# Layer 0, second pass: score blocks above the diagonal loaded as 32-squares to their transposed place and turned by VectorE

## The chip, the cores and the metric

The kernel runs on one core of a Trainium2 chip. The metric is the device time of one execution in microseconds. A core has five engines that run their own instruction streams and wait for each other by semaphores: TensorE (PE, with PEld for its weight loads), VectorE (DVE), ScalarE (ACT), GpSimd (POOL) and SyncE (SP). Transfers run on 16 DMA engines; SP and POOL issue them. SBUF and PSUM are the on-chip memories; TensorE writes PSUM.

## The reference

Two graph layers, one after the other, on a feature array `x` of 4096 x 512 with a 4096 x 4096 adjacency `adj`. The change is in the first. Cut to what matters:

```python
h = jnp.maximum(_layernorm(x), 0.0)
node_att = softmax(h @ node_w, axis=0)
he = h @ edge_w
e = he @ he.T                              # 4096 x 4096 scores, symmetric
e = jnp.where(adj > 0, e, NEG_BIG)
edge_att = softmax(e, axis=1)
output = adj * (node_att * edge_att) @ (h @ weight)
x = x + output + bias
# then layer 1: a graph attention layer with 8 heads of 64, same N and adj
```

Everything is 32-bit floating point. The scores before the mask are symmetric: `e` and its transpose are the same array.

## The kernel before, in words

With P = 128 rows to a tile there are NT = 32 row tiles; BL = 512 columns make a block, NB = 8 blocks, TB = 4 tiles in a block.

**First pass** (to about 707 us). Score tiles are computed for blocks on and above the diagonal only (L285), and each 128 x 512 tile `es` is written to an HBM array `e_d` (L289, issued by POOL). Row maxima are collected for the softmax. The lower half of `e_d` is never written.

**Second pass** (about 707 to 1650 us, `load`, `turn`, `exps`, `weigh`, `gather`). It loops over blocks b of 512 output rows and, inside, over the 32 row tiles m of neighbours. A step (b, m) needs the scores with neighbours on the partitions: the 128 x 512 tile whose rows are the neighbours of tile m and whose columns are the outputs of block b. Where m lies left of the block (m // 4 < b) this tile is in `e_d` as it stands and is loaded as `et` (L350). On the diagonal (m // 4 == b) a trapezoid of four parts is loaded into `eb` (L346), and what is missing is turned by TensorE. Right of the block (m // 4 > b, "above the diagonal") only the transposed block exists: one DMA loads 512 x 512 scores for four steps into `eb` (L354), and in each of those steps TensorE turns four 128 x 128 tiles into a PSUM tile `pt` (L370).

- `load(b, m)`, 8 steps ahead: the DMAs above, all on SP's queue, and that of the adjacency tile `a` (L358).
- `turn(b, m)`, 3 ahead: the transposes.
- `exps(b, m)`, 2 ahead: VectorE makes a mask `mk` from `a` (L378), subtracts the row maxima `mb` from the scores (L381, from PSUM or SBUF to `d`) and adds the mask (L382); ScalarE takes the exponential (L384).
- `weigh(b, m)`, 1 ahead: VectorE multiplies by the adjacency into `at` (L390); GpSimd adds up the row sum `racc` (L400).
- `gather(b, m)`, 0 ahead: TensorE multiplies `at` into the four PSUM accumulators `po` (L420), eight matmul instructions a step[...].

The order is written out by hand: for every step the stages are recorded in this sequence, so on each engine and each queue the instructions stand in this order and are executed in it. Pools set how far a stage can run ahead: `eb` has 4 buffers, `a` 11, `pt` 3 PSUM banks, `at` 3. A DMA on SP's queue waits, before it is issued, for the buffer it fills and for the DMA issued eight before it. At the end of the pass the next layer's preparation is mixed into row block 7, which has no step above the diagonal.

**Layer 1** (from about 1650 us) does not touch what is changed.

Of the kernel before, what the change touches and what calls it, by code (L numbers as in the profile page):

```python
# [8 lines left out]
FP = mybir.dt.float32  # L9
AF = mybir.ActivationFunctionType  # L10
ALU = mybir.AluOpType
# [4 lines left out]
P = 128  # L16
# [6 lines left out]
def row_bcast(ap, n, offset=0):  # L23

    return bass.AP(tensor=ap.tensor, offset=ap.offset + offset, ap=[[0, P], [1, n]])
# [3 lines left out]
def kernel(  # L29
# [15 lines left out]
    nc = tc.nc  # L45
    N, F = x.shape
# [5 lines left out]
    BL = 512  # L52
    NB = N // BL
    TB = BL // P

    const = ctx.enter_context(tc.tile_pool(name="const", bufs=1))
    dram = ctx.enter_context(tc.tile_pool(name="dram", bufs=1, space=DRAM))
# [13 lines left out]

    e_d = dram.tile([N, N], FP, name="e_d")
    mx_d = [dram.tile([TB, P], FP, name=f"mx_d{b}") for b in range(NB)]
    xb_d = dram.tile([N, F], FP, name="xb_d")
    big = ctx.enter_context(tc.tile_pool(name="l0", bufs=1))
# [19 lines left out]
    with tc.tile_pool(name="w0", bufs=1) as wp, tc.tile_pool(name="a0", bufs=2) as ap_, tc.tile_pool(  # L97
        name="a0s", bufs=8
# [38 lines left out]
        def turn(t):  # L137
            b, j = divmod(t, TB)
            if j == 0:
                hts[b] = ap_.tile([P, KC, BL], FP, name="h_t")  # L140
            h = hs.pop(t)
            pt = pp.tile([P, KC, P], FP, name="pt")
            for k in range(KC):
                nc.tensor.transpose(pt[:, k, :], h[:, k * P:(k + 1) * P], ident)  # L144
            nc.vector.tensor_copy(hts[b][:, :, j * P:(j + 1) * P], pt)
            hw = sp.tile([P, F], FP, name="hw", bufs=1)
            nc.vector.tensor_tensor_reduce(hw, h, nw_b, 1.0, 0.0, ALU.mult, ALU.add, lg[:, t:t + 1])
            xb = sp.tile([P, F], FP, name="xb", bufs=1)
            nc.gpsimd.tensor_tensor(xb, xts.pop(t), bias_b, ALU.add)
            nc.gpsimd.dma_start(xb_d[t * P:(t + 1) * P, :], xb)  # L150
# [92 lines left out]
    with tc.tile_pool(name="mx", bufs=1) as mxp, tc.tile_pool(name="b_a", bufs=6) as adjp, tc.tile_pool(  # L243
        name="b_e", bufs=4
    ) as esp, tc.tile_pool(name="b_m", bufs=2) as mkp, tc.tile_pool(name="b_s", bufs=2) as sp, tc.tile_pool(
        name="b_p", bufs=6, space=PSUM
# [11 lines left out]
        def load(i, j, t):  # L258
            w, lo, sk = parts(i, j, t)
            rows = slice(t * P, (t + 1) * P)  # L260
            ar = adjp.tile([P, BL], FP, name="ar")
            nc.sync.dma_start(ar[:, :w], adj[rows, lo:lo + w])
            ac = None
            if w > sk:
                ac = adjp.tile([P, BL], FP, name="ac")
                nc.sync.dma_start(ac[:, sk:w], adj_t[rows, lo + sk:lo + w])
            loaded[i, j, t] = ar, ac
# [35 lines left out]
        for n in range(-6, len(items)):  # L303
# [3 lines left out]
            if n >= 0:  # L307
                i, j, t = items[n]
# [9 lines left out]
    with tc.tile_pool(name="c_a", bufs=11) as adjp, tc.tile_pool(name="c_b", bufs=4) as ebp, tc.tile_pool(  # L318
        name="c_e", bufs=9
    ) as etp, tc.tile_pool(name="c_w", bufs=3) as wkp, tc.tile_pool(name="c_t", bufs=3) as atp, tc.tile_pool(  # L320
        name="c_m", bufs=2
    ) as mxp, tc.tile_pool(name="c_o", bufs=4) as iop, tc.tile_pool(name="c_s", bufs=2) as sp, tc.tile_pool(
        name="c_p", bufs=1, space=PSUM
    ) as p_o, tc.tile_pool(name="c_q", bufs=3, space=PSUM) as p_t, tc.tile_pool(
        name="c_r", bufs=1, space=PSUM
    ) as p_r, tc.manual_schedule():
        steps = [(b, m) for b in range(NB) for m in range(NT)]
        blk = {}
        src, aj, ex, at = {}, {}, {}, {}

        def rows_of(m):
            return slice(m * P, (m + 1) * P)

        def load(b, m):
            cols = slice(b * BL, (b + 1) * BL)
            if m == 0:
                mb = mxp.tile([P, BL], FP, name="mb") if b else mb_0
                if b:
                    nc.gpsimd.dma_start(mb, row_bcast(mx_d[b], BL))
                blk[b] = [mb, None, None, None]  # L340
            if m // TB == b:
                if m % TB == 0:
                    eb = ebp.tile([P, TB, BL], FP, name="eb")
                    for i in range(TB):
                        q = (m + i) * P
                        nc.sync.dma_start(eb[:, i, i * P:], e_d[q:q + P, q:(b + 1) * BL])  # L346
                        src[b, m + i] = eb
            elif m // TB < b:
                et = etp.tile([P, BL], FP, name="et")
                nc.sync.dma_start(et, e_d[rows_of(m), cols])  # L350
                src[b, m] = et
            elif m % TB == 0:
                eb = ebp.tile([P, TB, BL], FP, name="eb")
                nc.sync.dma_start(eb, e_d[cols, m * P:m * P + BL].rearrange("(j p) f -> p j f", p=P))  # L354
                for i in range(TB):
                    src[b, m + i] = eb
            a = adjp.tile([P, BL], FP, name="a")
            nc.sync.dma_start(a, adj_t[rows_of(m), cols])  # L358
            aj[b, m] = a

        def turn(b, m):

            i = m % TB
            n = TB if m // TB > b else i if m // TB == b else 0
            eb = src[b, m]
            parts = []
            if n > 0:
                pt = p_t.tile([P, BL], FP, name="pt")
                for j in range(n):
                    nc.tensor.transpose(pt[:, j * P:(j + 1) * P], eb[:, j, i * P:(i + 1) * P], ident)  # L370
                parts.append((slice(0, n * P), pt))
            if n < TB:
                parts.append((slice(n * P, BL), eb[:, i, :] if m // TB == b else eb))
            src[b, m] = parts

        def exps(b, m):
            mk = wkp.tile([P, BL], FP, name="mk")
            nc.vector.tensor_scalar(mk, aj[b, m], 0.0, NEG_BIG, ALU.is_le, ALU.mult)  # L378
            d = wkp.tile([P, BL], FP, name="d")
            for cs, part in src.pop((b, m)):  # L380
                nc.vector.tensor_tensor(d[:, cs], part[:, cs], blk[b][0][:, cs], ALU.subtract)  # L381
            nc.vector.tensor_tensor(d, d, mk, ALU.add)  # L382
            e = wkp.tile([P, BL], FP, name="ex")
            nc.scalar.activation(e, d, AF.Exp)  # L384
            ex[b, m] = e
# [44 lines left out]
        def finish():  # L430

            t, acc, oc, rs, xt = left.pop(0)
            b, j = divmod(t, TB)
            if j == 0:
                sc = sp.tile([P, TB], FP, name="sc")
                nc.vector.reciprocal(sc, rs)
                nc.vector.tensor_tensor(sc, sc, na[:, b * TB:(b + 1) * TB], ALU.mult)
                scale[b] = sc
            nc.vector.scalar_tensor_tensor(oc, acc, scale[b][:, j:j + 1], xt, op0=ALU.mult, op1=ALU.add)
            nc.gpsimd.dma_start(x1[rows_of(t), :], oc)  # L440
# [71 lines left out]
        end = len(steps)  # L512

        def tail(s):

            if s == -6:
                w_fetch()
            if -6 <= s and s + 6 < NT:
                fetch(s + 6)
            if s == -2:  # L520
                stats(0)
                stats(1)
                norm(0)
                stats(2)
                norm(1)
            if s >= 0:
                if 0 < s:
                    values(s - 1)
                if s + 2 < NT:
                    norm(s + 2)  # L530
                if s + 3 < NT:
                    stats(s + 3)
                if s == 0:
                    turn_h(0)
                if s + 1 < NT:
                    turn_h(s + 1)
                linear(s)
                if s > 1:
                    logits(s - 2)
                if s == WT + 2:  # L540

                    pt = p_t.tile([P, BL], FP, name="pt")
                    for h in range(HG):
                        nc.tensor.transpose(pt[:WT, h * P:(h + 1) * P], s_n[:, h, 0:WT], ident)
                    st = sp.tile([WT, HG, P], FP, name="s_t", bufs=1)
                    nc.vector.tensor_copy(st.rearrange("t h p -> t (h p)"), pt[:WT, :])
                    nc.gpsimd.dma_start(s_d.rearrange("h t p -> t h p"), st)

        stages = ((load, 8), (turn, 3), (exps, 2), (weigh, 1), (gather, 0))
        for s in range(-8, end):  # L550
            for f, ahead in stages:
                if 0 <= s + ahead < end:
                    f(*steps[s + ahead])
                if f is weigh:
                    if left and s % NT > 1:
                        finish()
                    tail(s - end)
                    if s == 3:
                        ending = maxima(NB - 1, acc_z, p_t, sp)
                    if s in (3, 4):  # L560
                        next(ending, None)
# [10 lines left out]
        pt = p_t.tile([P, BL], FP, name="pt")  # L572
# [50 lines left out]
    with tc.tile_pool(name="p", bufs=2) as prp, tc.tile_pool(name="rl", bufs=2) as rlp, tc.tile_pool(  # L623
        name="io1", bufs=3
    ) as iop, tc.tile_pool(name="s1", bufs=1) as sp, tc.tile_pool(name="za", bufs=1) as zp0, tc.tile_pool(name="e3", bufs=2) as e3p, tc.tile_pool(
        name="zb", bufs=1
    ) as zp1, tc.tile_pool(name="e", bufs=3) as ep, tc.tile_pool(name="ac", bufs=2) as acp, tc.tile_pool(
        name="os", bufs=1
    ) as osp, tc.tile_pool(name="u", bufs=1) as usp, tc.tile_pool(
        name="p_x", bufs=1, space=PSUM  # L630
    ) as p_x, tc.tile_pool(name="p_v", bufs=1, space=PSUM) as p_v, tc.tile_pool(
        name="p_t1", bufs=1, space=PSUM
# [4 lines left out]
        zs_, ra, ex, e3, rl, pr, acc, pv, late = {}, {}, {}, {}, {}, {}, {}, {}, {}  # L637
# [307 lines left out]
        stages = ((load, 3), (logs, 5), (exps, 1), (weigh, 1), (factors, 2), (scale, 2), (gather, 0))  # L945
# [47 lines left out]
```

## Time and profile before

| | |
|---|---|
| median of 3 runs | 3022.19 us (3020.59 to 3024.23) |
| the profiled execution | 3021.79 us |
| its span, first to last instruction | 3020.0 us |
| granted TensorE clock, mean | 0.995 |
| TensorE busy | 2978.9 us, 99% of the span |
| VectorE busy | 2485.5 us, 82% |
| transposes of L370 (diagonal blocks included) | 496 |
| loads of L354, 1 MB each | 28, landing after 5.9 us (median) |
| SP's DMA queue (q1) | 179,056 packets, 387.79 MB, 39.5% of the 16 DMA engines' span |

The page of a profile lists busy times of the engines, 40 slices of the span, the DMA queues, the chain of work that ended last (followed back from the last instruction to what released each), and the costliest groups of instructions. A group's row reads: line, engine, operation, output<-inputs, shapes, count | total busy us, mean ns of one | idle us of the engine just before them, and what ended most of it. A packet is one contiguous piece of a transfer, or the few bytes by which a DMA reports that it is done; a queue's share is the time that its packets took, out of 16 engines times the stretch. Every view can be asked for a stretch of the span.

### The profile page before, as it was taken

The page shows a single profiled execution, that of the slowest core. Times are in us where ns is not written, and L with a number is a line of the kernel's source. Part 1 is how long each engine was busy: PE and PEld are TensorE (multiplying, and loading weights), DVE is VectorE, ACT ScalarE, POOL GpSimd, SP SyncE. Part 2 cuts the span into 40 slices and gives each one's busy share as a digit, 9 for nine tenths or more (in the row PEclk, how much of TensorE's full clock was granted, in tenths as well). Part 3 has the DMA queues.
Part 4 walks back from the last instruction along what each step waited for, and adds up shares of the span by engine and source line. Part 5 has one row for each costly group of instructions (what it writes and reads, how often), then busy time and mean ns, then how long its engine had stood idle before and what let it go on. Part 6 is the DMA issues. An engine that isn't in the chain of part 4 may idle for free.

```text
span 3020.0 us, 43197 instructions
## 1 busy us (share of the span) xinstructions
PE 2978.9 (99%) x15819; PEld 1207.6 (40%) x15819; DVE 2485.5 (82%) x3484; ACT 1326.2 (44%) x1852; POOL 1361.8 (45%) x1042
## 2 busy tenths in 40 slices
PE   8999999999999999999999989999999999999998
PEld 4444444444444444444444432323222322232222
DVE  5435777777677686887987779999999999999998
ACT  2111111111111121112122358888777777777776
POOL 3401111113333343443544656575756575757574
PEclk9999999999999999999999999999999999999999
DMA  4205667766455454554554228797979797979795
GB/s 153 98 4 195 222 220 223 233 211 222 138 167 159 146 168 137 177 175 134 189 165 131 67 88 214 214 232 207 236 213 231 213 237 213 230 217 234 214 230 156
DMA packets 232293, 551.99 MB, mean 183 GB/s; under 512 B 25528, under 2 KB 51160, under 8 KB 232080
## 3 DMA queue, kind: packets, MB, share of 16 engines
q1 hardware_dynamic: 179056, 387.79, 39.5%
q0 software_dynamic: 51008, 157.51, 22.6%
q10 hardware_dynamic: 2016, 3.93, 0.4%
q8 instruction: 124, 2.03, 0.3%
q14 instruction: 89, 0.73, 0.1%
HBM read 409.47 MB, written 59.97 MB: 155 GB/s over the span
## 4 chain that ended last, share of the span: by engine, by line
PE 91%; DVE 4%; ACT 2%; DMA 1%; issue 1%; POOL 0%; SPq 0%; DVEq 0%; ACTq 0%; POOLq 0%
PE po L420 29%; PE pv L773 24%; PE pe L285 15%; PE dn L778 8%; PE po L490 4%; PE ps L156 4%; PE pe L163 4%; DVE pr L741 3%; PE pt L370 2%; DMA acc<-pr 1%; PE pt L828 1%; DVE pr L738 1%; ACT e L709 1%; PE pt L144 0%; PE pt L482 0%
## 5 line engine op out<-in xcount | busy, mean ns | idle before, releaser
L773 PE MATMUL pv<-pr,sup 128*32 128x512 f32 x8192 | 1009.8, 594 | 10.3 <-POOL d_m L938 5.6
L420 PE MATMUL po<-sup,at 128*128 128x512 f32 x2048 | 904.5, 594 | 2.8 <-DVE at L390 2.8
L750 POOL TENSOR_TENSOR acc<-acc,pr 128x1024 f32<-128x1024 f32 x232 | 558.9, 2409 | 316.5 <-DVE pr L741 316.0
L741 DVE SCALAR_TENSOR_TENSOR pr<-z,g_m,ex 128x1024 f32<-128x1024 f32 x512 | 630.7, 1272 | 6.0 <-ACT ex L699 5.9
L420 PEld LDWEIGHTS po<-sup,at 128*128 128x128 f32 x2048 | 378.6, 190 | 428.0 <-issue 416.6
L400 POOL TENSOR_TENSOR racc<-racc,ex 128x512 f32<-128x512 f32 x240 | 343.6, 1432 | 450.6 <-ACT ex L384 449.3
L773 PEld LDWEIGHTS pv<-pr,sup 128*32 128x32 f32 x8192 | 291.3, 110 | 589.4 <-issue 532.4
L384 ACT ACTIVATE ex<-d 128x512 f32<-128x512 f32 x256 | 160.6, 630 | 721.9 <-DVE d L382 714.1
L285 PE MATMUL pe<-he_t,he_t 128*128 128x512 f32 x896 | 386.4, 592 | 0.0
L699 ACT ACTIVATE ex<-e 128x1024 f32<-128x1024 f32 x256 | 263.0, 1028 | 227.9 <-DVE pr L741 227.7
L741 DVE SCALAR_TENSOR_TENSOR pr<-z,g_m,e 128x1024 f32<-128x1024 f32 x256 | 328.7, 1284 | 10.0 <-PE pv L773 5.8
L778 PE MATMUL dn<-pr,d_m 128*2 128x512 f32 x1984 | 334.7, 592 | 0.0
L709 ACT ACTIVATE e<-e,ld_m 128x1024 f32<-128x1024 f32 x256 | 291.0, 1137 | 5.0 <-DMA e<-in_adj_t_dram 4.6
L738 DVE SCALAR_TENSOR_TENSOR pr<-rl,ngd_m,ex 128x1024 f32<-128x1024 f32 x224 | 284.8, 1271 | 1.6 <-ACT ex L699 1.2
L382 DVE TENSOR_TENSOR d<-d,mk 128x512 f32<-128x512 f32 x256 | 269.9, 1054 | 8.8
L727 ACT ACTIVATE rl<-z,ngd_m,d_m 128x1024 f32<-128x1024 f32 x224 | 275.1, 1228 | 0.0
L285 PEld LDWEIGHTS pe<-he_t,he_t 128*128 128x128 f32 x896 | 169.2, 190 | 210.1 <-issue 190.5
L288 ACT COPY es<-pe 128x512 f32<-128x512 f32 (+2 forms) x144 | 79.3, 550 | 377.0 <-PE pe L285 377.0
L289 POOL DMA_DIRECT2D e_d<-es x144 | 78.6, 546 | 364.6 <-ACT es L288 359.0
L381 DVE TENSOR_TENSOR d<-pt,mb 128x512 f32<-128x512 f32 (+2 forms) x136 | 87.4, 643 | 165.6 <-PE pt L370 165.6
L390 DVE TENSOR_TENSOR at<-ex,a 128x512 f32<-128x512 f32 x256 | 175.5, 686 | 23.2 <-ACT ex L384 21.3
L290 DVE CUSTOM_DVE_ANT_0 mk<-pe,mk 128x512 f32<-128x512 f32 (+2 forms) x144 | 93.0, 646 | 99.2 <-ACT es L288 99.2
(172 smaller groups left out, 2650.1 us busy)
## 6 DMA issues: line engine op xcount, KB each, us to landing
e<-in_adj_t_dram SPq DMA_DIRECT2D x256, 512.0 KB, 5.5
acc<-pr POOLq DMA_DIRECT2D x152, 512.0 KB, 5.9
a<-in_adj_t_dram SPq DMA_DIRECT2D x256, 256.0 KB, 3.2
ar<-in_adj_dram SPq DMA_DIRECT2D x120, 256.0 KB, 3.4
e_d<-es POOLq DMA_DIRECT2D x120, 256.0 KB, 3.3
ac<-in_adj_t_dram SPq DMA_DIRECT2D x112, 256.0 KB, 4.0
eb<-e_d SPq DMA_DIRECT2D x28, 1024.0 KB, 5.9
et<-e_d SPq DMA_DIRECT2D x112, 256.0 KB, 3.3
```

What stands on the lines that cost most here:

```text
L285: nc.tensor.matmul(pe[:, :w], he_t[i][:, k, (t % TB) * P:(t % TB + 1) * P], he_t[j][:, k, BL - w:], start=(k == 0), stop=(k == KC - 1))
L382: nc.vector.tensor_tensor(d, d, mk, ALU.add)
L400: nc.gpsimd.tensor_tensor(racc, racc, e, ALU.add)
L420: nc.tensor.matmul(po[j], w[:, j * P:(j + 1) * P], sup[:, m, :], start=(m == 0), stop=last)
L699: nc.scalar.activation(x_, ra.pop((i, m)), AF.Exp)
L709: nc.scalar.activation(x_, ra[i, m], AF.Exp, bias=ld_m[:, h // HG, m:m + 1])
L727: nc.scalar.activation(r, zs_[i, 0], AF.Relu, bias=ngd_m[:, h // HG, m:m + 1], scale=d_m[:, h, m:m + 1])
L738: nc.vector.scalar_tensor_tensor(w, rl.pop((i, m)), ngd_m[:, h // HG, m:m + 1], x_, op0=ALU.subtract, op1=ALU.mult)
L741: nc.vector.scalar_tensor_tensor(w, zs_[i, k], g_m[:, h + k, m:m + 1], e3.pop((i, m)) if k == 3 else x_, op0=ALU.max, op1=ALU.mult)
L750: nc.gpsimd.tensor_tensor(acc[i, 3], acc[i, 3], w, ALU.add)
L773: nc.tensor.matmul(v[c][q][r * D + c0:r * D + c0 + Q, :], va[:, m, g * HG + k, c0:c0 + Q], pr[i, m, k][:, q * BL:(q + 1) * BL], start=(m = ...
L778: nc.tensor.matmul(dn[r * Q:r * Q + w.shape[1], :], w, src[:, q * BL:(q + 1) * BL], **fl)
```

## The change

For blocks above the diagonal the one load of 512 x 512 scores becomes 16 loads on SP's queue. Each takes, for one row tile i and one group c of 32 neighbour columns, all 512 output rows as 16 groups of 32, and puts every 32 x 32 square at the place that its transpose has in the 128 x 512 tile: 32 partitions, 16 squares side by side, each piece 32 numbers (128 bytes) long. What is left is to turn each square in itself, which one VectorE transpose of 128 x 512 per step does, from SBUF into the PSUM tile `pt`. These loads stand in a stage of their own, `squares`, 11 steps ahead instead of 8.

Two more edits go with it. The subtraction of the maxima now writes `pt` in place (or into `pt` from SBUF, for steps not above the diagonal), and the addition of the mask reads `pt` instead of `d`; `pt` is allocated in every step. The rows of `e_d` in HBM are 64 numbers (256 bytes) longer.

```diff
+    S = 32
-    e_d = dram.tile([N, N], FP, name="e_d")
+    e_d = dram.tile([N, N + 2 * S], FP, name="e_d")[:, 0:N]
...
         def load(b, m):
...
-            elif m % TB == 0:
-                eb = ebp.tile([P, TB, BL], FP, name="eb")
-                nc.sync.dma_start(eb, e_d[cols, m * P:m * P + BL].rearrange("(j p) f -> p j f", p=P))
-                for i in range(TB):
-                    src[b, m + i] = eb
...
+        def squares(b, m):
+            cols = slice(b * BL, (b + 1) * BL)
+            if m // TB > b and m % TB == 0:
+                eb = ebp.tile([P, TB, BL], FP, name="eb")
+                sq = e_d[cols, m * P:m * P + BL].rearrange("(a p) (i c q) -> i c p a q", p=S, q=S, i=TB)
+                for i in range(TB):
+                    for c in range(P // S):
+                        nc.sync.dma_start(eb[c * S:(c + 1) * S, i, :].rearrange("p (a q) -> p a q", q=S), sq[i, c])
+                for i in range(TB):
+                    src[b, m + i] = eb
...
         def turn(b, m):
-            n = TB if m // TB > b else i if m // TB == b else 0
+            pt = p_t.tile([P, BL], FP, name="pt")
+            pts[b, m] = pt
+            if m // TB > b:
+                nc.vector.transpose(pt, eb[:, i, :])
+                src[b, m] = [(slice(0, BL), pt)]
+                return
+            n = i if m // TB == b else 0
...
         def exps(b, m):
...
-                nc.vector.tensor_tensor(d[:, cs], part[:, cs], blk[b][0][:, cs], ALU.subtract)
-            nc.vector.tensor_tensor(d, d, mk, ALU.add)
+                nc.vector.tensor_tensor(pt[:, cs], part[:, cs], blk[b][0][:, cs], ALU.subtract)
+            nc.vector.tensor_tensor(d, pt, mk, ALU.add)
...
-        stages = ((load, 8), (turn, 3), (exps, 2), (weigh, 1), (gather, 0))
-        for s in range(-8, end):
+        stages = ((squares, 11), (load, 8), (turn, 3), (exps, 2), (weigh, 1), (gather, 0))
+        for s in range(-11, end):
```

More of the change, by code (lines that the diff above doesn't have):

```diff
@@ L328 @@
         blk = {}
-        src, aj, ex, at = {}, {}, {}, {}
+        src, pts, aj, ex, at = {}, {}, {}, {}, {}
         def rows_of(m):
@@ L359, in load @@
             aj[b, m] = a
+        def squares(b, m):
[8 more added lines that the diff above has]
+                    src[b, m + i] = eb
         def turn(b, m):
             i = m % TB
-            n = TB if m // TB > b else i if m // TB == b else 0
             eb = src[b, m]
+            pt = p_t.tile([P, BL], FP, name="pt")
+            pts[b, m] = pt
             parts = []
+            if m // TB > b:
[3 more added lines that the diff above has]
+            n = i if m // TB == b else 0
             if n > 0:
-                pt = p_t.tile([P, BL], FP, name="pt")
                 for j in range(n):
@@ L379, in exps @@
             d = wkp.tile([P, BL], FP, name="d")
+            pt = pts.pop((b, m))
             for cs, part in src.pop((b, m)):
-                nc.vector.tensor_tensor(d[:, cs], part[:, cs], blk[b][0][:, cs], ALU.subtract)
-            nc.vector.tensor_tensor(d, d, mk, ALU.add)
+                nc.vector.tensor_tensor(pt[:, cs], part[:, cs], blk[b][0][:, cs], ALU.subtract)
+            nc.vector.tensor_tensor(d, pt, mk, ALU.add)
             e = wkp.tile([P, BL], FP, name="ex")
```

## The prediction

> **What bounds the kernel now.** I read the page first: the busy row, then the chain that ended last.
>
> ```profile
> PE 2978.9 (99%) x15819; PEld 1207.6 (40%) x15819; DVE 2485.5 (82%) x3484; ACT 1326.2 (44%) x1852; POOL 1361.8 (45%) x1042
> PE 91%; DVE 4%; ACT 2%; DMA 1%; issue 1%; POOL 0%; SPq 0%; DVEq 0%; ACTq 0%; POOLq 0%
> ```
>
> TensorE is the path almost everywhere, so an instruction taken off it should shorten the end, unless another resource of the same stage then needs longer. The stage is the second pass of layer 0, some 707 to 1650 us. The chain for 757 to 815 us, all of it above the diagonal in row 0, shows its beat:
>
> ```profile
> 760.56 3.44 PE po L420 x8
> 764.00 0.44 PE pt L370 x4
> 764.43 3.44 PE po L420 x8
> 767.87 0.44 PE pt L370 x4
> ```
>
> A step is eight matmul instructions of L420 (3.44 us) and, above the diagonal, four transposes of L370 (0.44 us); nothing else is in the chain. The start of the step recurs every 3.87 us. What the other engines do in that beat, the groups of the stretch 757 to 818 us say:
>
> ```profile
> L382 DVE TENSOR_TENSOR d<-d,mk 128x512 f32<-128x512 f32 x16 | 11.1, 692 | 0.5
> L381 DVE TENSOR_TENSOR d<-pt,mb 128x512 f32<-128x512 f32 x16 | 11.1, 692 | 24.3 <-PE pt L370 24.3
> L390 DVE TENSOR_TENSOR at<-ex,a 128x512 f32<-128x512 f32 x16 | 10.9, 684 | 0.0
> L378 DVE TENSOR_SCALAR mk<-a 128x512 f32<-128x512 f32 x16 | 6.7, 419 | 0.0
> ```
>
> VectorE works 692 + 692 + 684 + 419 = 2487 ns a step and then waits for the transposes (24.3 us in 16 steps). The busy row by stages gives 757 to 815 us a DMA share of 0.44 at 139 GB/s. So two budgets matter after the change: a step of 3.44 us for VectorE, and four steps, 13.75 us, for the transfers of one block of four.
>
> [...] The trace before has no VectorE transpose.
>
> **The change, part by part.**
>
> *Removed from TensorE.* Above the diagonal are 28+24+20+16+12+8+4 = 112 steps, each with four transposes. 112 x 0.437 us (3.872 less 3.436) = **-48.9 us**, all of it on the path. The 48 transposes in the diagonal blocks stay.
>
> *Added to VectorE.* One transpose of 128x512 a step. Price: [...] about 0.685 us (estimate). Bounds: 0.42 us (the one-source mask, L378)[...]. The subtraction now writes PSUM and the addition reads PSUM. The row closest to both is L381 from PSUM, 692 ns; a write into PSUM is not shown, so 0.69 us, between 0.6 and 1.2. A step is then 2.49 + 0.685 = 3.17 us, 92% of 3.44: hidden behind L420, with 0.26 us to spare. If that cover goes, the excess falls 112 times on the path. Below the diagonal the addition, 1054 ns on average because it reads two SBUF tiles beside GpSimd, should get shorter; TensorE covers both, so it is worth nothing.
>
> *Changed in the transfers.* A 1 MB block was one DMA of 512 pieces of 2 KB. It becomes 16 DMAs of 512 pieces of 128 B: 8192 pieces, 512 on each of 16 DMA engines. The price of a short piece can be read from two stretches that hold hardly anything else. First, 1.4 to 2.3 us, where q1 carries one load of 128 pieces of 16 B with 16 completion packets; second, 628.1 to 628.7 us, a load of 128 pieces of 512 B with 16 completions:
>
> ```profile
> q1 hardware_dynamic: 144, 0.00, 7.8%
> ```
>
> ```profile
> DMA packets 145, 0.07 MB, mean 109 GB/s; under 512 B 17, under 2 KB 145, under 8 KB 145
> q1 hardware_dynamic: 144, 0.07, 37.0%
> ```
>
> 7.8% of 16 x 0.9 us is 1.12 us, 7.8 ns a packet. 37.0% of 16 x 0.6 us is 3.55 us; less 16 completions, 26.8 ns for 512 B. On the line between them 128 B cost 7.8 + 112 x 0.0383 = 12.1 ns. I take that; the upper end is 26.8 ns, since nothing suggests that a shorter piece takes longer. Block: 512 x 12.1 ns = 6.2 us. The four adjacency tiles beside it: 32 pieces of 2 KB an engine at 100 ns (42.6% of 16 x 58 us on q1 for 7.74 MB) = 3.2 us. Together 9.4 us of 13.75: covered, share about 0.7. At 26.8 ns it is 16.9 us and not covered.
>
> *The queue on SP.* 16 issues instead of one. Four L346 issues take 1.75 us, 0.44 each, so 7.0 us a block and 8.8 us with the four loads: below 13.75. Each issue also waits for the DMA eight before it; at a landing of 2 to 3 us for small loads, eight in flight allow one every 0.4 us. The squares are issued three steps earlier than the block was, and four `eb` buffers hold three blocks ahead, so a late landing has some 40 us. They are released now by VectorE's transpose instead of TensorE's, at the same step.
>
> *What stands behind them.* The load of `a` for step 1 was issued right after step 0's (699.3 us); now the first squares stand between, 16 x 0.5 us. It lands near 711 us, where the timeline has its mask at 709.1 us. VectorE needs it before `at` of step 0, for which TensorE waits at 711.6: **+2.5 us** (0 to 7). Later loads have six steps in hand. POOL's queue, ScalarE and the padded row pitch (a wider stride, the same bytes): nothing, no instruction is added there.
>
> Sum: -48.9 + 2.5 = -46.4. The profiled execution took 3021.8 us (span 3020.0), 0.4 below the median of 3022.2, so the two can be exchanged: **2975 us**.
>
> **The rivals.**
>
> *VectorE becomes the bound.* For: 92% of the step leaves little, and neither its transpose nor its writes into PSUM are in this trace. [...] With a transpose of 1.22 us the step is 3.71 us, 0.27 too long: 112 x 0.27 = 30 back, about **3005 us**. With the subtraction at 1.2 us as well, 4.2 us, it would be slower than before; both at once are unlikely.
>
> *Transfers are late, but little.* At 26.8 ns a block is 3.2 us late. Row 0 has seven blocks and a lead of about 10 us (12 lost), row 1 rebuilds part of its lead in eight steps without squares (6 lost), later rows have enough; the first squares hold up `a` by 7. About **3000 us**.
>
> *Slower: short pieces scattered over rows cost more than the line says.* Above 26.8 ns each further ns adds 0.512 us to some 18 blocks of rows 0 to 2, 9 us. The gain is used up near 30 ns. At 40 ns, with 22 blocks late, some 160 us are lost: **about 3130 us**, with the DMA share at 1.0 and TensorE waiting in rows 0 to 3. For: every 128 B come from another row 16 KB away, and the 16 B load was one contiguous stretch. Against: the 512 B loads also stride whole rows, and 26.8 ns is less than 30.
>
> *The change doesn't do what it says.* The built order excludes it: above the diagonal one VectorE transpose of 128x512 stands where four on TensorE stood.
>
> **How the numbers follow.** Covered, -55 to -36 us: 0.68 (from no cost at the start and 6 us, one measurement's spread, below the sum, to the 7 us and a few short waits). VectorE or transfers part-way, 2986 to 3014 us: 0.12. The two about cancel, within 0.2% (6 us, about what a measurement of this kernel can tell from none): 0.04. Slower: 0.16, nearly all of it the price of short pieces, some of it VectorE. Range 2966 to 3014 us: the first two cases, with the bounds of the unknown prices. Faster 0.80, same 0.04, slower 0.16.
>
> **What would show it.** Right: the chain above the diagonal is L420 alone with 3.44 us a step; a VectorE transpose group x112 near 0.69 us; VectorE near 3.2 us a step; DMA share about 0.7 where squares run, q1 up by some 220,000 packets. Wrong: TensorE idle before L420 with the releaser behind it VectorE's transpose waiting for `eb` (price of pieces, the stretch at share 1.0), or VectorE without idle at more than 3.44 us a step (transpose or PSUM writes). A start of row 0 more than 7 us late would refute the +2.5.

## The result, and the profile after

| | before | after |
|---|---|---|
| median of 4 runs each | 3023.21 us (3020.59 to 3024.98) | 2992.59 us (2991.55 to 2993.92) |
| the profiled execution | 3021.79 us | 2991.82 us |

The ratio is 0.99, 95% interval 0.9883 to 0.9917: 30.6 us faster where 46.4 were forecast. The direction and the range held; some 16 us of the expected gain are missing. The page of the kernel after, its busy row and the row of its chain of waits:

```profile
PE 2942.8 (98%) x15371; PEld 1155.0 (39%) x15371; DVE 2607.1 (87%) x3596; ACT 1325.5 (44%) x1852; POOL 1340.9 (45%) x1042
...
PE 76%; DVE 11%; DMA 4%; SPq 3%; issue 3%; ACT 2%; POOL 0%; DVEq 0%; ACTq 0%; POOLq 0%
```

TensorE has the 448 matmul records less (15,819 to 15,371), so the work went away as planned. But it holds only 76% of the chain where it had 91%, and VectorE has 11% where it had 4%. VectorE's busy time grew by 122 us; 112 transposes at 718 ns are 80 us of it. So other VectorE instructions became longer. Which ones, the busy times of the stretch 757 to 815 us (all above the diagonal in row 0) and VectorE's groups there show. The columns of the first are stretch, its length, busy us of PE, PEld, DVE, ACT and POOL, the granted clock, the DMA share and GB/s:

```profile
757.00:815.00 58.00, 57.40 (x127) 22.88 (x127) 57.48 (x79) 9.82 (x16) 21.05 (x17) 1.00 0.80 186
```

```profile
L392 DVE TENSOR_SCALAR mk<-a 128x512 f32<-128x512 f32 x16 | 19.5, 1217 | 0.0
L378 DVE STREAM_TRANSPOSE pt<-eb 128x512 f32<-128x512 f32 x16 | 11.5, 718 | 0.0
L396 DVE TENSOR_TENSOR pt<-pt,mb 128x512 f32<-128x512 f32 x16 | 11.0, 685 | 0.0
L405 DVE TENSOR_TENSOR at<-ex,a 128x512 f32<-128x512 f32 x16 | 10.9, 681 | 0.0
L397 DVE TENSOR_TENSOR d<-pt,mk 128x512 f32<-128x512 f32 x15 | 10.4, 691 | 0.5
```

VectorE is busy for 57.48 of 58 us, with next to no idle in front of its groups (last column, 0.5 us in all). Its transpose and its operations on PSUM cost 0.69 to 0.72 us each. The mask of L392, which the change leaves alone, takes **1217 ns, where it took 419 before**. TensorE now waits once in every step, for 12.6 us in this stretch. From the waits of the stretch (total, times, longest):

```profile
PEld po L435 <- DVE at L405: 12.6, 16, 0.9
```

What the mask ran beside, the timelines of VectorE and of GpSimd for 801 to 806 us tell (start, us, engine and line, operation):

```profile
800.66 0.68 DVE L405 TENSOR_TENSOR at<-ex,a 128x512 f32<-128x512 f32 x1
801.26 0.72 DVE L378 STREAM_TRANSPOSE pt<-eb 128x512 f32<-128x512 f32 x1
801.89 1.27 DVE L392 TENSOR_SCALAR mk<-a 128x512 f32<-128x512 f32 x1
803.08 0.69 DVE L396 TENSOR_TENSOR pt<-pt,mb 128x512 f32<-128x512 f32 x1
803.80 0.69 DVE L397 TENSOR_TENSOR d<-pt,mk 128x512 f32<-128x512 f32 x1
804.41 0.68 DVE L405 TENSOR_TENSOR at<-ex,a 128x512 f32<-128x512 f32 x1
```

```profile
801.61 1.27 POOL L415 TENSOR_TENSOR racc<-racc,ex 128x512 f32<-128x512 f32 x1 [2.48 <-ACT ex L399]
```

`at` recurs after 3.75 us, not 3.44: that is VectorE's step. In it the mask starts at 801.89, while GpSimd's row sum `racc` already runs, and ends at 803.16, 0.28 us after `racc` has ended (802.88). In the kernel before, the mask of this stretch was over before `racc` began:

```profile
770.28 0.42 DVE L378 TENSOR_SCALAR mk<-a 128x512 f32<-128x512 f32 x1
770.92 1.27 POOL L400 TENSOR_TENSOR racc<-racc,ex 128x512 f32<-128x512 f32 x1 [2.90 <-ACT ex L384]
```

ScalarE's exponential releases `racc` about 1 us after the start of VectorE's `at` (0.95 us here, 1.24 in the kernel before). The transpose has been put between `at` and the mask, and so pushed the mask into `racc`.

### The profile page after: what moved, and what is told of

It reads as the page before. It is cut to its first block, busy times and chain, and to the rows that moved or that the text cites. A ratio compares the mean times of both kernels' runs of the same rounds, so it can differ in the third digit from the quotient of the medians.

```text
span 2990.0 us, 43039 instructions
## 1 busy us (share of the span) xinstructions
PE 2942.8 (98%) x15371; PEld 1155.0 (39%) x15371; DVE 2607.1 (87%) x3596; ACT 1325.5 (44%) x1852; POOL 1340.9 (45%) x1042
## 4 chain that ended last, share of the span: by engine, by line
PE 76%; DVE 11%; DMA 4%; SPq 3%; issue 3%; ACT 2%; POOL 0%; DVEq 0%; ACTq 0%; POOLq 0%
PE pv L788 22%; PE po L435 18%; PE pe L288 15%; PE dn L793 7%; PE ps L159 4%; PE po L505 4%; PE pe L166 4%; DVE pr L756 4%; SPq L366 3%; DVE mk L392 2%; DMA acc<-pr 2%; DVE at L405 2%; DVE pt L396 1%; DVE pt L378 1%; DMA eb<-e_d 1%
## 5 line engine op out<-in xcount | busy, mean ns | idle before, releaser
L435 PE MATMUL po<-sup,at 128*128 128x512 f32 x2048 | 899.7, 596 | 8.8 <-DVE at L405 6.8
L435 PEld LDWEIGHTS po<-sup,at 128*128 128x128 f32 x2048 | 383.2, 190 | 504.4 <-issue 435.6
L415 POOL TENSOR_TENSOR racc<-racc,ex 128x512 f32<-128x512 f32 x240 | 323.5, 1348 | 457.9 <-ACT ex L399 455.9
L392 DVE TENSOR_SCALAR mk<-a 128x512 f32<-128x512 f32 x256 | 219.3, 857 | 3.8 <-DMA a<-in_adj_t_dram 3.8
L405 DVE TENSOR_TENSOR at<-ex,a 128x512 f32<-128x512 f32 x256 | 193.5, 756 | 13.9 <-ACT ex L399 9.5
L397 DVE TENSOR_TENSOR d<-pt,mk 128x512 f32<-128x512 f32 x256 | 176.9, 691 | 8.9
```

The source lines that it names most:

```text
L415: nc.gpsimd.tensor_tensor(racc, racc, e, ALU.add)
L435: nc.tensor.matmul(po[j], w[:, j * P:(j + 1) * P], sup[:, m, :], start=(m == 0), stop=last)
```

## The experiments

Two theories stood at the start. **M**: the mask, stretched beside GpSimd's row sum, makes VectorE the bound of a step, that is, what sets its length. **T**: the squares come late (the chain names SP's queue at L366 with 3%, and q1 rose to a share near 0.8), and VectorE only waits for them or for SP. Apart from both stood the longer start. All times are medians; the ratio is to the kernel before, run on the same chip. Beside e1 to e4 the kernel before took 3021.85 us, 1.4 less than beside the kernel after (3023.21), so what these four gain over the change is known to some 1.5 us. e5 to e7 ran beside 3023.13 us.

### e1: the mask made after the subtraction, above the diagonal

```diff
@@ exps(b, m)
-            nc.vector.tensor_scalar(mk, aj[b, m], 0.0, NEG_BIG, ALU.is_le, ALU.mult)
+            late_mask = m // TB > b
+            if not late_mask:
+                nc.vector.tensor_scalar(mk, aj[b, m], 0.0, NEG_BIG, ALU.is_le, ALU.mult)
...
                 nc.vector.tensor_tensor(pt[:, cs], part[:, cs], blk[b][0][:, cs], ALU.subtract)
+            if late_mask:
+                nc.vector.tensor_scalar(mk, aj[b, m], 0.0, NEG_BIG, ALU.is_le, ALU.mult)
```

> Same work as the changed kernel; above the diagonal the mask is made after the subtraction instead of before it, so that it no longer runs beside GpSimd's row sum. Theory M (VectorE is the bound above the diagonal because the mask is stretched from 0.42 to 1.19 us by GpSimd's addition that runs beside it): the mask returns to 0.42 us there, a step of VectorE takes 3.0 to 3.15 us, TensorE's beat above the diagonal returns to 3.43 us, rows 0 to 3 lose their 14 us: about 2978 us. Theory T (the squares land late and hold up TensorE): nothing that is late gets earlier, 2990 to 2994 us.

Measured: 2977.08 us, ratio 0.9853 (0.9838 to 0.9867), so 15.5 us less than the change alone. The chain of waits of 757 to 815 us is one piece of TensorE, in the beat that was predicted (137 matmul records in 58.8 us, 3.43 us for eight):

```profile
756.59 58.80 PE po L439 x137
```

The mask did not come down to 0.42 us, though: it took 712 ns on average. The timelines of VectorE and GpSimd at 764 us show why:

```profile
764.00 0.67 DVE L398 TENSOR_TENSOR pt<-pt,mb 128x512 f32<-128x512 f32 x1
764.58 0.69 DVE L400 TENSOR_SCALAR mk<-a 128x512 f32<-128x512 f32 x1
```

```profile
763.72 1.26 POOL L419 TENSOR_TENSOR racc<-racc,ex 128x512 f32<-128x512 f32 x1 [1.87 <-ACT ex L403]
```

The subtraction lies wholly beside `racc` and keeps its 0.67 us; it reads one tile from PSUM and one from SBUF. The mask again ends 0.29 us after `racc` (765.27 against 764.98), as it did in the kernel after, whenever it starts: the next two, at 767.72 and 770.86 us, take 0.70 and 0.98 us and end 0.30 and 0.29 us after theirs. At the new place less of `racc` is left when the mask starts. VectorE's step is then 3.14 us here (765.91 to 769.05 for `at`) and hidden again behind TensorE's 3.43.

### e2: GpSimd's row sums left out above the diagonal

```diff
@@ weigh(b, m)
                 nc.gpsimd.tensor_tensor(racc, ex.pop((b, 0)), e, ALU.add)
+                nc.gpsimd.tensor_scalar(racc, racc, 1.0, None, ALU.add)
-            else:
+            elif m // TB <= b:
```

> The changed kernel with GpSimd's row sums left out above the diagonal (from the third step of a row on), one constant added per row so that no sum is zero; the outputs are not the reference's. Theory M: with nothing beside it on GpSimd the mask takes 0.42 us, beat 3.43 us, about 2978 us. If something else stretches the mask (transfers that write SBUF), it stays near 1.2 us and the time near 2992 us. Theory T: 2990 to 2994 us.

Measured: 2978.7 us, ratio 0.9854 (0.9837 to 0.987). The order on VectorE is that of the change; only its neighbour is gone, and the mask is back at its old price in VectorE's groups of 757 to 815 us:

```profile
L392 DVE TENSOR_SCALAR mk<-a 128x512 f32<-128x512 f32 x17 | 7.0, 410 | 3.3 <-DMA a<-in_adj_t_dram 3.3
```

VectorE waits for a load of `a` there, but TensorE's chain of this stretch is again one piece. The edit takes 13.9 us off, about what moving the mask does (15.5), in a wholly different way. So it is the meeting of the two that costs, and not the mask's place or the transpose in front of it.

### e3: the squares issued 8 steps ahead, as the block was

```diff
-        stages = ((squares, 11), (load, 8), (turn, 3), (exps, 2), (weigh, 1), (gather, 0))
-        for s in range(-11, end):
+        stages = ((squares, 8), (load, 8), (turn, 3), (exps, 2), (weigh, 1), (gather, 0))
+        for s in range(-8, end):
```

> The changed kernel with the squares issued 8 steps ahead instead of 11, so that the loads of a for steps 1 to 3 stand before the first squares again. Theory M: only the start gains, TensorE begins the pass 4 us earlier, rows otherwise as in the changed kernel, about 2988 us. Theory T: with three steps less lead the squares are later, rows 0 to 2 get longer, 2995 to 3010 us.

Measured: 2987.27 us, ratio 0.9884 (0.987 to 0.9899): 5.3 us less than the change. It comes from the start. SP's queue, first in the kernel after:

```profile
698.25 1.75 SPq L349 DMA_DIRECT2D eb<-e_d  x4
700.05 0.43 SPq L356 DMA_DIRECT2D a<-in_adj_t_dram  x1
700.66 10.03 SPq L366 DMA_DIRECT2D eb<-e_d  x16
710.73 1.91 SPq L356 DMA_DIRECT2D a<-in_adj_t_dram  x4
```

and in this one:

```profile
699.36 1.92 SPq L356 DMA_DIRECT2D a<-in_adj_t_dram  x4
701.76 11.35 SPq L366 DMA_DIRECT2D eb<-e_d  x16
```

In the kernel after, the second `a` stands behind sixteen squares and is issued at 710.73. VectorE's timeline shows what that does to step 1, and with it to `at` of step 0, which stands behind this mask:

```profile
713.92 0.43 DVE L392 TENSOR_SCALAR mk<-a 128x512 f32<-128x512 f32 x1 [3.79 <-DMA a<-in_adj_t_dram]
```

With the squares behind the first four `a`, TensorE's first L435 starts at 712.0 us instead of 716.5. The squares still come in time (from 757 to 1000 us VectorE waits for none), and the mask still takes 1216 ns: this edit does nothing for the stretched mask.

### e4: one load of 2 KB pieces again, VectorE still turns

```diff
-                sq = e_d[cols, m * P:m * P + BL].rearrange("(a p) (i c q) -> i c p a q", p=S, q=S, i=TB)
-                for i in range(TB):
-                    for c in range(P // S):
-                        nc.sync.dma_start(eb[c * S:(c + 1) * S, i, :].rearrange("p (a q) -> p a q", q=S), sq[i, c])
+                nc.sync.dma_start(eb, e_d[cols, m * P:m * P + BL].rearrange("(j p) f -> p j f", p=P))
```

> The changed kernel with the 16 loads of squares of a block put back to the one load of 2 KB pieces of the kernel before (11 steps ahead); VectorE still turns, so the scores above the diagonal are in wrong places and the outputs are not the reference's. Theory M: VectorE's beat of 3.75 us above the diagonal stays, only the 4 us at the start come back, about 2988 us. Theory T: all of the loss is gone, 2972 to 2978 us.

Measured: 2987.12 us, ratio 0.9883 (0.9869 to 0.9898), 5.5 us less than the change, of which 2.8 are a shorter start (first L435 at 713.7 us). The short pieces are gone, the DMA share of 757 to 815 us is back at 0.45, and VectorE's groups and the busy times say the same of VectorE as with them:

```profile
L389 DVE TENSOR_SCALAR mk<-a 128x512 f32<-128x512 f32 x16 | 19.5, 1216 | 0.0
```

```profile
757.00:815.00 58.00, 57.62 (x130) 23.74 (x129) 57.44 (x79) 9.50 (x16) 21.05 (x17) 1.00 0.45 143
```

VectorE is busy for 57.44 of 58 us with no squares at all. T is rejected, and the 3% of SP's queue in the chain of the kernel after were no cause: taking the squares away left the 3.75 us step as it was.

### e5: both, the mask late and the squares 8 ahead

The edit is that of e1 and that of e3 together.

> Both edits at once: the mask after the subtraction above the diagonal, and the squares 8 steps ahead. Theory M: the two losses are separate and add up, so the 14 us of the beat and the 4 to 5 us of the start both come back: about 2972 us, TensorE starts the pass near 711.9 us and rows 1 to 7 take 111.4 to 112.4 us. If the faster beat needs the three steps of lead (theory T at this beat), rows 0 and 1 get longer than with the mask alone: 2977 us or more.

Measured: **2973.79 us, ratio 0.9837 (0.9824 to 0.9851)**, 49.3 us under the kernel before (3023.13 on the same chip) and 18.8 under the change: the fastest version, ahead of both kernels. Its page:

```profile
PE 2930.5 (99%) x15371; PEld 1168.0 (39%) x15371; DVE 2548.9 (86%) x3596; ACT 1325.4 (45%) x1852; POOL 1346.6 (45%) x1042
...
PE 87%; DVE 5%; DMA 3%; ACT 2%; issue 2%; POOL 0%; SPq 0%; DVEq 0%; ACTq 0%; POOLq 0%
```

TensorE has most of its share of the chain back, VectorE's busy time fell by 58 us without one instruction less, and SP's queue has left the chain.

### e6: e1 with the score array's row pitch not padded

```diff
-    e_d = dram.tile([N, N + 2 * S], FP, name="e_d")[:, 0:N]
+    e_d = dram.tile([N, N], FP, name="e_d")
```

> The kernel with the mask moved, with the rows of e_d 16 KB apart as before the change, without the 256 bytes of padding. If the pitch doesn't matter, a 128-byte piece keeps its price of about 14 ns on a DMA engine and the time stays 2977 us. If 512 pieces at a pitch of 16 KB collide in HBM, the price rises; above some 20 to 25 ns the transfers become the bound in rows 0 and 1, with TensorE waiting for the squares there: 2985 to 3050 us.

Measured: 2976.63 us, ratio 0.9848 (0.9835 to 0.9861), beside e1's 2977.08 (0.9853). The padding is worth nothing that can be measured here. As TensorE waits for no transfer from 757 to 815 us, in e1 or here, the time alone would hide a small difference; the price of the squares would not, and it is much the same with padding and without. Here is q1's row of 757 to 815 us (packets, MB, share of 16 engines), first e1, then e6:

```profile
q1 hardware_dynamic: 35591, 11.85, 86.9%
```

```profile
q1 hardware_dynamic: 37019, 12.01, 89.6%
```

That is 22.7 and 22.5 ns a packet over nearly the same mixture. The trace's own packet records give a 128 B piece 13.54 ns on average in e1 and 13.55 in e6.

### e7: the kernel before, with the subtraction into PSUM alone

```diff
@@ turn(b, m), every step
+            pt = p_t.tile([P, BL], FP, name="pt")
+            pts[b, m] = pt
@@ exps(b, m)
-                nc.vector.tensor_tensor(d[:, cs], part[:, cs], blk[b][0][:, cs], ALU.subtract)
-            nc.vector.tensor_tensor(d, d, mk, ALU.add)
+                nc.vector.tensor_tensor(pt[:, cs], part[:, cs], blk[b][0][:, cs], ALU.subtract)
+            nc.vector.tensor_tensor(d, pt, mk, ALU.add)
```

> The kernel before, with one part of the change alone: the subtraction writes pt in PSUM and the addition of the mask reads it; loads and transposes as before. The addition falls from 1054 to about 691 ns on average, the subtraction stays near 0.69 us from PSUM. Theory M: TensorE is the bound everywhere in that kernel, so nothing changes, within 3 us of the kernel before. If writing PSUM by VectorE cost more than writing SBUF, it would be in L381's row.

Measured: 3022.93 us, ratio 0.9999 (0.9991 to 1.0007): no effect on the time. The groups of VectorE in 707 to 1650 us:

```profile
L384 DVE TENSOR_TENSOR d<-pt,mk 128x512 f32<-128x512 f32 x256 | 176.9, 691 | 8.8
...
L383 DVE TENSOR_TENSOR pt<-et,mb 128x512 f32<-128x512 f32 x112 | 121.1, 1081 | 0.0
```

The addition takes 690 to 693 ns in all 256 steps, as it now reads one tile from PSUM; of two SBUF tiles it took 1054 on average. The subtraction of two SBUF tiles below the diagonal takes 1081 ns where it took 813. In the kernel before:

```profile
L382 DVE TENSOR_TENSOR d<-d,mk 128x512 f32<-128x512 f32 x256 | 269.9, 1054 | 8.8
L381 DVE TENSOR_TENSOR d<-et,mb 128x512 f32<-128x512 f32 x112 | 91.1, 813 | 0.0
```

The addition is 93 us cheaper in all, and this subtraction 30 us dearer; the masks are 20 us dearer and `at` 17. So a good part of what the addition paid beside GpSimd is now paid by the instructions that have come to stand there. None of it reaches the time, since TensorE covers it.

## Why the prediction was right, and where it was not

**TensorE, -48.9 us: right.** The instructions went, and in e5, where mask and start are mended, the time fell by 49.3 us. That the two figures are so close is partly chance. In the profiles the second pass of e5, from the first L439 to the last row sums, is 47.7 us shorter than in the kernel before (712.7 to 1603.6 us against 711.6 to 1650.2); the rest is a start 1.1 us later and a tail 2.0 us shorter.

**"A step is then 2.49 + 0.685 = 3.17 us ... hidden behind L420": this is the step that failed.** The measured step was 3.75 us, above TensorE's 3.44. The other durations came out close to the forecast: 718 ns for the transpose (685, the author's estimate, as the trace before had no such transpose), 685 for the subtraction into PSUM (692), 691 for the addition from it (692), 681 for `at` (684). The mask took 1217 ns for 419: its price was taken from a place where nothing ran beside it, and kept at a place where `racc` did.

The sum itself hid part of this. It adds durations, but in the timeline above an instruction starts up to 0.09 us before the one before it has ended. From start to start, the step at 800.66 us is 0.60 (`at`), 0.63 (transpose), 1.19 (mask), 0.72 and 0.61, together 3.75. Earlier in the same trace, where GpSimd's addition begins only at 716.77 us, as the mask ends, the instruction behind the mask starts 0.34 us after it:

```profile
716.39 0.42 DVE L392 TENSOR_SCALAR mk<-a 128x512 f32<-128x512 f32 x1
716.73 0.42 DVE L396 TENSOR_TENSOR pt<-pt,mb 128x256 f32<-128x256 f32 x1
```

With that the step would be some 2.90 us, not 3.17. The meeting with `racc` thus adds 0.85 us to it, and 0.31 of these stand above TensorE's beat.

The prediction had the collision in its hands. It said of the addition below the diagonal that it takes 1054 ns "because it reads two SBUF tiles beside GpSimd", but asked this of no instruction that changed its neighbour. (The 1054 is the mean of all 256 steps; as those above the diagonal took 692, it was some 1.34 us in the others.)

What it cost is the difference between the change and e1: 15.5 us. The matmuls of the row sums at the end of each row place it. The first number after the durations is the end of row 0, the second that of the last row, first in the kernel after, then in e1:

```profile
L432 PEld LDWEIGHTS rs<-ones,racc x64: 190/192/192, 830.4 to 1622.8; 128*128 128x128 f32 x64
L436 PEld LDWEIGHTS rs<-ones,racc x64: 190/192/193, 824.7 to 1606.7; 128*128 128x128 f32 x64
```

Row 0 ends 5.7 us later than in e1 (830.4 against 824.7; 0.4 of it is a later start), row 1 13.4 later (950.5 against 937.1), row 2 15.5 (1064.0 against 1048.5), the last 16.1. So the loss falls in rows 0 to 2, with 28, 24 and 20 steps above the diagonal. An excess of 0.31 us in each of these would be 8.7, 7.4 and 6.2 us; the rows lost 5.7, 7.7 and 2.1, and all later rows together 0.6. A lead that VectorE gains in the steps at and before the diagonal would explain why the later rows lose nothing, but no run isolates it. The prediction had such a lead in its rival on transfers, but priced its VectorE rival at 112 steps.

**The rival "VectorE becomes the bound" had the right form with the wrong cause.** Its step of 3.71 us is near the measured 3.75; it was reached by a transpose of 1.22 us, which the author supposed and no trace had shown, and the transpose took 0.72. The sign named for it, VectorE without idle for more than 3.44 us a step, was seen, but its bracket "(transpose or PSUM writes)" was wrong. That the time fell inside the stated range is owed to this rival, in part by luck. The case called covered (-55 to -36 us, given 0.68) did not happen; the one with VectorE or transfers part-way (0.12) did, for a reason that it did not name. Had the excess of 0.31 us fallen on all 112 steps, as the rival counts them, 35 us would have been lost instead of 15.5.

**Start, +2.5 us: the mechanism right, the size short.** TensorE's first L435 moved from 711.6 to 716.5 us, inside the bounds of 0 to 7. Some of this is the spread of executions: the first pass ended 0.8 us later in this profile, and in e7, which changes no load, the first one starts at 713.3. The sixteen issues took 10.03 us, 0.63 each, where 0.5 was taken. e3 gives 5.3 us back, e5 over e1 3.3.

**Transfers: covered, as predicted.** The DMA share was 0.80 for 0.7. q1's packets rose by 221,760, from 179,056 to 400,816. In the kernel after, q1's row of 757 to 815 us reads

```profile
q1 hardware_dynamic: 32306, 10.46, 78.8%
```

78.8% of 16 x 58 us over 32,306 packets is 22.6 ns for the mixture; the trace's own packet records give 13.5 ns for a 128 B piece, against 12.1. In e1, at the faster beat, the share is 0.88 and still no transfer is waited for. The price that carried most of the chance for "slower" was close to the line drawn through two other stretches.

**The sum.** -48.9, +15.5 and +4.9 make -28.5 us; measured -30.6. The rest of 2 us fits a shorter tail: from the last row-sum weights to the end of the span it is 1369.8 us before and 1367.2 after. But it is 1369.6 in e3 and 1367.1 in e4, which have the same layer 1 as the kernel after, so this much varies between executions and need not come from the change.

## What to carry to other kernels

A duration read from a trace belongs to its neighbours too: before an instruction is put in front of others on an engine, look at what every instruction behind it will then run beside, and price again those that come to stand beside GpSimd (here the mask, 0.42 us alone and 1.22 beside `racc`). When a chain names a queue, take the queue's load away before believing it. If an engine is to be filled to 92% of the beat, a cheap reordering of its own instructions (here one line moved, 15.5 us) can be worth about a third of the whole gain.

## What the runs showed of the hardware that was not expected

- **A mask of 0.42 us became 1.22 us beside GpSimd's addition**, and ended 0.28 to 0.29 us after it. It has one SBUF source and a constant, and its 0.42 us is shorter than the 0.68 to 0.69 of the two-source operations. The subtraction with a PSUM source stays at 0.67 us under `racc`. The runs show which instructions stretch and when, not why.
- Operations with two SBUF sources stretched as well: the subtraction below the diagonal took 0.69 us at its median and 1.77 at most in e7 (in the kernel after, 1.76 at 1591.75 us, where `racc` had begun at 1591.52). The addition with one source in PSUM kept to 690 to 693 ns in all 256 steps.
- A 32x32-square transpose of 128x512 by VectorE from SBUF into PSUM took 718 ns, some 30 more than the two-source operations of that size (681 to 692).
- A row pitch of 16 KB or of 256 B more made no difference to pieces of 128 B (e1 and e6: 13.54 and 13.55 ns a piece, 2977.08 and 2976.63 us).
